# Two 32x32-block transposes moved past the inner product's additions, and three PSUM tiles at the end made smaller

## The chip, the cores and the metric

The kernel runs on one core of one Trainium2 chip, in one launch. The metric is the device time of one execution in microseconds. The kernel before took 2105.44 us, the median of three runs (2105.36 to 2105.63). Engines are named as the profile names them: PE is TensorE, DVE is VectorE, ACT is ScalarE, POOL is GpSimd and SP is SyncE, which issues the loads and stores here. PEld is PE's weight load.

## What is computed

Two layers on x (16 batches, 1024 nodes, 256 channels) in f32, with one adjacency matrix of 1024 by 1024 for all batches:

```python
# layer 0
c_adj = jnp.mean(fea, axis=1)                      # fea: x with channels first
diff = c_adj[:, None, :] - c_adj[:, :, None]
A = jnp.abs(jnp.abs(jax.nn.sigmoid(diff) - 0.5) - 0.5) * 2.0
A_s = (A + jnp.transpose(A, (0, 2, 1))) * 0.5
g = jax.nn.relu(jnp.einsum('bcn,bnm->bcm', fea, adj[None] * A_s) * para.reshape(1, C, N))
# q from g, k and v from x @ kv_w, 4 heads of 64
attn = jax.nn.softmax(jnp.einsum('bhnd,bhmd->bhnm', q, k) * scale, axis=-1)
x = _layernorm(x + jnp.einsum('bhnm,bhmd->bhnd', attn, v))
# layer 1, twice: loop + neighbours, 256 -> 128 -> 256
h = jax.nn.relu(x @ w1_loop + adj @ (x @ w1_neigh) + b1)
h = jax.nn.relu(h @ w2_loop + adj @ (h @ w2_neigh) + b2)
x = _layernorm(x + (x + h) * 0.5)
```

## The kernel before

One Python loop over the 16 batches lays out all instructions. The order on each engine is the order of the code, which is written by hand: there is no planner. What a tile waits for follows from its data and from its buffer: tiles of one tag take that tag's buffers in turn, and the next owner of a buffer waits until the last one has been read. PSUM has two tags: "big" (`big_psum`, L85, three buffers of two banks; `half_psum`, L88, takes one and uses half of it) and "bank" (`bank_psum`, L91, two buffers of one bank).

The batches are staggered. While batch b is in its attention, the first graph convolution runs for batch b - 1 (the object `c1`), the second for b - 2 (`c2`), and the last normalization for b - 3 (`c3`). Batches 2 to 14 share one branch (L1590 to L1649). Batches 3 to 14 have a `c3`; batch 2 has none. Batch 15 has its own branch (L1651 and L1731 on), as no batch follows it. After the loop, one more run and the ending serve what is left (from L1741).

In batches 2 to 14 the stage around the change goes like this:

- `att.both_units(0, ...)` (L828): scores of the first two of four units (PE, L769), exps (ACT, L776), their sums over the nodes (`collect`, DVE, L788 and L790), the products with v (PE, L815). The DVE part at its end, `settle`, is handed back and done later: a transpose of an av tile out of PSUM (L848) and a reduction (`part_sum`, L803). The function `summed` puts four sums (L1024 to L1027) and, where there is a `c3`, `deviation_aside` (DVE L1234, then POOL L1235, a power) ahead of that.
- `c1.fast_inner(...)` (L1032): x1 times the first layer's weights by Strassen's scheme with seven products of 128 by 512 on PE (L1037), in the order 1, 2, 7, 6, 3, 4, 5. They go to three half-used big PSUM tiles: `chain` takes 1, 6 and 5, `upper` takes 2 and 3, `lower` takes 7 and 4. ACT copies some of them out (L1043 to L1052), and DVE adds the others: L1045 reads `upper` after product 2, so product 3 waits for it; L1054 reads `lower` after product 4; L1056 and L1057 read `chain`; L1058 transposes the result, which SP then stores. Between L1045 and L1054 DVE does what `fast_inner` is handed as `aside`: `settle` and `turn_next`, the turn of next x from blocked to channel-major form, two transposes of 128x1024 (L253 in `channel_major`).
- `att.both_units(1, ...)`: the other two units in the same way. Its first score tiles take the big buffers that `upper`, `lower` and `chain` had, so the second of them waits for L1054. `third` of this call issues the ACT copy L880 behind its `settle`.
- `Joined.run` (L1385): both graph convolutions' products with the adjacency, also seven of them, in the order 1, 2, 6, 7, 5, 4, 3, with DVE work for other batches put between by `between`.

In batch 15 `fast_inner` has only `settle` as its `aside`. Its joined run ends with `c2.last_products` (L1181), seven products of which L1189 and L1196 add parts and `settle` (L1176, the line L1178) adds results to x. Its `between` puts `norm.scale` (L393, two DVE multiplications) behind product 4 and `norm.spread` (L395) behind product 3's relu: two transposes of x1 to channel-major form (L253) and eight stores of 128 KB each. L1449 is the addition that the relu (L1076) waits for. Then `c1.turn(0)` and `c1.turn(1)` turn h1 on PE (four transposes of 128x128 each, L1109) into a half-used big tile, and ACT copies it out (L1110). The last run begins with `c1.inner` for batch 15 (L1006), whose 32 products go to another big tile (L1011, `t_ps`) and are copied by ACT (L1014).

Of the kernel before, what the change touches and what calls it, by code (L numbers as in the profile page):

```python
# [10 lines left out]
F32 = mybir.dt.float32  # L11
# [7 lines left out]
def kernel(  # L19
# [31 lines left out]
    nc = tc.nc  # L51

    B, N, C = x.shape
    P = 128
    NT = N // P
    NC = C // P
# [22 lines left out]
    work = ctx.enter_context(tc.tile_pool(name="work", bufs=1))  # L79
# [169 lines left out]
    def channel_major(blocked, name):  # L249

        dst = work.tile([P, NC, N], F32, tag="xT", name=name, bufs=2)
        for cc in range(NC):
            nc.vector.transpose(dst[:, cc, :], blocked[cc])  # L253
        return dst
# [103 lines left out]
    class BlockedNorm:  # L358
# [31 lines left out]
        def scale(self):  # L390
            for cc in range(NC):
                x_cc = by_node(self.xB[cc])
                nc.vector.tensor_mul(x_cc, x_cc, self.rstd.unsqueeze(2).to_broadcast([P, NB, S]))  # L393

        def spread(self):  # L395
            self.x1T = channel_major(self.xB, f"x1T_{self.name}")
            self.nodes = nodes = dram.tile([N, C], F32, tag="x1d", name=f"x1d_{self.name}", bufs=3)
            for cc in range(NC):
                for a in range(Q):
                    c0 = cc * P + a * S  # L400
                    nc.sync.dma_start(out=nodes[:, c0:c0 + S].rearrange("(bn k) r -> k bn r", k=S),
                                      in_=by_node(self.xB[cc][a * S:(a + 1) * S, :]))
# [591 lines left out]
    class GraphConv:  # L994
# [34 lines left out]
            self.inner_factors = {1: (w1n_sb[:, 0, :], w11), 2: (w1n_sb[:, 1, :], w21), 3: (s4, w22),  # L1029
                                  4: (w1l_sb[:, 1, :], t4), 5: (s1, t1), 6: (s2, t2), 7: (s3, t3)}  # L1030

        def fast_inner(self, aside=lambda: None):  # L1032
            b = self.b

            def product(n, dst, again=False):
                w, xs = self.inner_factors[n]
                nc.tensor.matmul(dst, w, xs, start=not again, stop=True, skip_group_check=again)  # L1037

            upper, lower, chain = (half_psum(f"in_ps_{b}_{i}") for i in range(3))
            s12, s34, t1T, self.loops, t1B = (row_tile(f"in_{b}_{i}") for i in range(5))  # L1040
            p1, u2, p3, p7 = s12[:, 0:FB], s12[:, FB:N], s34[:, 0:FB], s34[:, FB:N]
            product(1, chain)
            nc.scalar.copy(p1, chain)  # L1043
            product(2, upper)
            nc.vector.tensor_add(t1T[:, 0:FB], p1, upper)  # L1045
            aside()
            product(7, lower)
            nc.scalar.copy(p7, lower)
            product(6, chain, again=True)
            nc.scalar.copy(u2, chain)  # L1050
            product(3, upper)
            nc.scalar.copy(p3, upper)  # L1052
            product(4, lower, again=True)
            nc.vector.tensor_add(self.loops[:, 0:FB], u2, lower)  # L1054
            product(5, chain, again=True)
            nc.vector.tensor_add(t1T[:, FB:N], p3, chain)  # L1056
            nc.vector.tensor_add(self.loops[:, FB:N], p7, chain)  # L1057
            nc.vector.transpose(t1B, t1T)  # L1058
            self.t1d = dram.tile([N, HID], F32, tag="t1d", name=f"t1d_{b}", bufs=2)
            for a in range(Q):  # L1060
                nc.sync.dma_start(out=self.t1d[:, a * S:(a + 1) * S].rearrange("(bn k) r -> k bn r", k=S),
                                  in_=by_node(t1B[a * S:(a + 1) * S, :]))
# [115 lines left out]
            nc.vector.scalar_tensor_tensor(rows, src.rearrange("p (t c) -> p t c", c=P), 0.0, rows,  # L1178
                                           op0=ALU.max, op1=ALU.add)

        def last_products(self, a, c):  # L1181
            name = f"h2_{self.b}"
            d = bank_psum(f"{name}_ps")
            snaps = [row_tile(f"{name}_{k}") for k in range(2)]
            p1, u2, u3 = snaps[0][:, 0:FB], snaps[0][:, FB:N], snaps[1][:, 0:FB]
            self.seventh_part(1, a)
            nc.scalar.copy(p1, a)
            self.seventh_part(2, d, start=True)
            nc.vector.tensor_add(p1, p1, d)  # L1189
            self.settle(0, 0, p1)  # L1190
            self.seventh_part(6, a)
            nc.scalar.copy(u2, a)
            self.seventh_part(5, c)
            self.seventh_part(7, a)
            nc.scalar.copy(u3, a)
            nc.vector.tensor_add(u3, u3, c)  # L1196

            def rest():
                self.settle(1, 1, u3)
                self.seventh_part(4, a)  # L1200
                self.settle(1, 0, a)
                self.seventh_part(3, c)
                nc.vector.tensor_add(u2, u2, c)
                self.settle(0, 1, u2)

            return rest
# [144 lines left out]
    class Joined:  # L1351
# [30 lines left out]
                nc.tensor.matmul(dst, self.x[n][:, k, :], of_rows(rows, k),  # L1382
                                 start=(start and k == 0), stop=(k == TJ - 1), skip_group_check=again)

        def run(self, between=None, last=None):  # L1385
            c1, c2, b = self.c1, self.c2, self.b
            between = between or {}

            def bias(bank, row):
                nc.scalar.copy(bank.rearrange("p (t c) -> p t c", c=P), row.unsqueeze(1).to_broadcast([P, TJ, P]))  # L1390

            def turn_to(n):
                for f in between.get(n, ()):
                    f()

            bigs = [big_psum(f"hu_ps_{b}_{i}") for i in range(3)]
            first, third, second = (big[:, 0:FB] for big in bigs)
            s12, s34 = (row_tile(f"snap_{b}_{k}") for k in range(2))
            p1, u1, u3, p7 = s12[:, 0:FB], s12[:, FB:N], s34[:, 0:FB], s34[:, FB:N]
            if c1.loops is None:  # L1400
                c1.loop(third, 0, start=True)
            else:
                nc.scalar.copy(third, c1.loops[:, 0:FB])
            self.product(1, first, start=True)
            nc.scalar.copy(p1, first)
            turn_to(1)
            self.product(2, third, again=c1.loops is not None)
            nc.vector.tensor_add(p1, p1, third)
            turn_to(2)
            if last and c2.w2 is None:  # L1410
                c2.load_sums()
            self.product(6, first, again=True)
            nc.scalar.copy(u1, first)
            c1.relu(0, p1)
            turn_to(6)
            self.product(7, second, start=True)
            nc.scalar.copy(p7, second)
            if last:
                bias(third, b2_sb[:, ts(0, P)])
            turn_to(7)  # L1420
            self.product(5, first, again=True)
            nc.scalar.copy(u3, first)
            turn_to(5)
            self.product(4, second, again=True)
            c2.uT = row_tile(f"uT_{c2.b}")
            add_upper = lambda: nc.vector.tensor_add(c2.uT[:, 0:FB], u1, second)
            add_lower = lambda: (last or nc.gpsimd).tensor_add(c2.uT[:, FB:N], u3, p7)
            if not last:
                add_upper()
                add_lower()  # L1430
                turn_to(4)
                c1.loop(first, 1, again=True)
                self.product(3, first, again=True)
                c1.relu(1, first)
                turn_to(3)
                return
            c2.block_sums(last, add_upper, add_lower)
            bias(second, c2.b2_step)
            turn_to(4)
            if c1.loops is None:  # L1440
                c1.loop(first, 1, again=True)
            self.product(3, first, again=True, steps=range(0, TJ // 2))
            rest = c2.last_products(third, second)
            self.product(3, first, again=True, steps=range(TJ // 2, TJ))
            if c1.loops is None:
                c1.relu(1, first)
            else:
                loop = c1.loops[:, FB:N]
                nc.vector.tensor_add(loop, loop, first)  # L1449
                c1.relu(1, loop)  # L1450
            turn_to(0)
            rest()
            turn_to(3)
            return third, second, bigs[1][:, FB:N], bigs[2][:, FB:N]

    def run():
# [59 lines left out]
        for b in range(B):  # L1516
# [73 lines left out]
            elif more:  # L1590
# [12 lines left out]
                    if c3:  # L1603
                        c3.deviation_aside()

                def turn_next():
                    nonlocal xT_next
                    xT_next = channel_major(blocked, f"xT_{b + 1}")

                xT_next = None  # L1610

# [8 lines left out]
                settle = att.both_units(0, sums, lambda: nodes.turn(), summed=summed)  # L1620
                nodes.line()
                nodes.row()
                c1.fast_inner(lambda: (settle(), turn_next()))
                att.both_units(1, before_convolution, third=lambda: (att.den_shift(), q.times_adj(0), q.times_adj(TJ), att.den_halves()))
                both.left(nc.gpsimd)
                q.left(nc.gpsimd, blocked)
# [103 lines left out]
            else:  # L1730
# [3 lines left out]
                both.left(nc.gpsimd)  # L1734
                both.fetch(1, 4, "11")
                both.run({1: (lambda: att.add_pairs(1), att.watch), 6: (norm.mean, norm.squares, norm.sum_squares),
                          5: (lambda: norm.variance(bank_psum),), 4: (norm.scale,), 0: (norm.spread,)}, last=nc.vector)
                c1.turn(0)
                c1.turn(1)
            convs[b] = GraphConv(b, norm.x1T, norm.nodes)  # L1740
        c1, c2, c3, c4 = (convs[B - k] for k in (1, 2, 3, 4))  # L1741
        both = Joined(c1, c2)
# [87 lines left out]
```

## Time and profile before

| | |
|---|---|
| median of three runs | 2105.44 us |
| the profiled execution: time, span | 2104.63 us, 2102.8 us |
| PE busy | 2090.7 us, 99% of the span |
| DVE busy | 1875.1 us, 89% |
| ACT busy | 1265.9 us, 60% |
| POOL busy | 425.5 us, 20% |
| mean granted PE clock | 0.999 |
| DMA | 364.99 MB, 174 GB/s |
| chain that ended last | PE 94%, DVE 4%, issue 1% |
| one 128x1024 transpose (L253) | 1.22 us, 62 of them |
| one batch of the steady part (b = 3 to 14) | 129.1 us |

The span reaches from the first to the last instruction that the profiler recorded; the execution's own time has 1.83 us around it. A row of the timeline gives start, length, engine, line, operation, the tile written and the tiles read with their shapes, how many instructions were put together in the row, and in brackets how long the engine was idle ahead of them and what ended the wait. Consecutive instructions overlap by some tenths of a microsecond, so that a row of two is shorter than twice one. A busy PE here means that a product is in its pipeline.

### The profile page before, as it was taken

The page shows a single profiled execution, that of the slowest core. Times are in us where ns is not written, and L with a number is a line of the kernel's source. Part 1 is how long each engine was busy: PE and PEld are TensorE (multiplying, and loading weights), DVE is VectorE, ACT ScalarE, POOL GpSimd, SP SyncE. Part 2 cuts the span into 40 slices and gives each one's busy share as a digit, 9 for nine tenths or more (in the row PEclk, how much of TensorE's full clock was granted, in tenths as well). Part 3 has the DMA queues.
Part 4 walks back from the last instruction along what each step waited for, and adds up shares of the span by engine and source line. Part 5 has one row for each costly group of instructions (what it writes and reads, how often), then busy time and mean ns, then how long its engine had stood idle before and what let it go on. Part 6 is the DMA issues. An engine that isn't in the chain of part 4 may idle for free.

```text
span 2102.8 us, 24938 instructions
## 1 busy us (share of the span) xinstructions
PE 2090.7 (99%) x8282; PEld 988.5 (47%) x8282; DVE 1875.1 (89%) x2238; ACT 1265.9 (60%) x2190; POOL 425.5 (20%) x444
## 2 busy tenths in 40 slices
PE   9999999999999999999999999999999999999998
PEld 5354434445354453544535444354443534445355
DVE  7899998989989899898998989899899998989875
ACT  5844575556756576565755757557575585655523
POOL 2011103122031221213122031220312203122022
PEclk9999999999999999999999999999999999999999
DMA  9495756766648776477864768656586674966455
GB/s 216 122 178 189 145 140 205 138 216 146 173 168 161 242 135 192 151 146 244 142 216 139 135 232 162 230 120 146 206 176 217 143 147 183 185 212 136 137 184 187
DMA packets 688695, 364.99 MB, mean 174 GB/s; under 512 B 550704, under 2 KB 629936, under 8 KB 688560
## 3 DMA queue, kind: packets, MB, share of 16 engines
q1 hardware_dynamic: 688288, 363.07, 66.8%
q8 instruction: 67, 1.10, 0.2%
q14 instruction: 68, 0.56, 0.1%
q10 hardware_dynamic: 272, 0.26, 0.0%
HBM read 305.46 MB, written 57.80 MB: 173 GB/s over the span
## 4 chain that ended last, share of the span: by engine, by line
PE 94%; DVE 4%; issue 1%; DMA 0%; ACT 0%; SPq 0%; DVEq 0%; POOLq 0%; POOL 0%
PE av L815 20%; PE s L769 20%; PE hu_ps L1382 17%; PE g_ps L714 16%; PE v_ps L475 5%; PE k_ps L471 5%; PE hu_ps L1174 4%; PE g_ps L633 3%; PE in_ps L1037 1%; DVE xT L253 1%; DVE den_part L803 1%; DVE acc L790 1%; PE h_ps L1085 1%; PE u_ps L1114 1%; PE h_ps L1174 1%
## 5 line engine op out<-in xcount | busy, mean ns | idle before, releaser
L790 DVE TENSOR_TENSOR acc<-acc,pr 128x1024 f32<-128x1024 f32 x384 | 481.3, 1253 | 34.0 <-ACT pr L776 0.5
L769 PE MATMUL s<-qT,kT 64*128 64x512 f32 x2048 | 452.2, 594 | 1.6 <-DVE in L1054 0.7
L815 PE MATMUL av<-pr,v 128*64 128x512 f32 x2048 | 447.0, 594 | 0.0
L776 ACT ACTIVATE pr<-s 128x1024 f32<-128x1024 f32 x392 | 392.7, 1119 | 60.0 <-PE s L769 60.0
L769 PEld LDWEIGHTS s<-qT,kT 64*128 64x128 f32 x2048 | 194.2, 187 | 247.1 <-issue 186.6
L815 PEld LDWEIGHTS av<-pr,v 128*64 128x64 f32 x2048 | 144.1, 137 | 297.3 <-issue 265.7
L1382 PE MATMUL hu_ps<-adj,R 128*128 128x512 f32 x480 | 213.6, 592 | 0.0
L625 DVE SCALAR_TENSOR_TENSOR wg<-wg,adj 128x1024 f32<-128x1024 f32 x128 | 167.9, 1350 | 3.6 <-ACT wg L620 3.6
L774 ACT ACTIVATE pr<-s 128x512 f32<-128x512 f32 x240 | 142.6, 705 | 0.0
L619 ACT ACTIVATE wg<-c_row,c_sums 128x1024 f32<-128x1024 f32 x120 | 139.4, 1162 | 3.0 <-DVE accB L797 1.0
L1382 PEld LDWEIGHTS hu_ps<-adj,R 128*128 128x128 f32 x480 | 90.0, 190 | 107.1 <-issue 105.7
L620 ACT ACTIVATE wg<-wg 128x1024 f32<-128x1024 f32 x128 | 135.4, 1057 | 4.1
L388 POOL TENSOR_TENSOR rstd<-rstd,neg_half 128x32 f32<-128x32 f32 x16 | 88.3, 5520 | 147.4 <-DVE rstd L385 146.3
L1235 POOL TENSOR_TENSOR rstd<-rstd,neg_half 128x8 f32<-128x8 f32 x12 | 19.7, 1640 | 440.4 <-DVE rstd L1234 440.4
L714 PE MATMUL g_ps<-wg,x 128*128 128x512 f32 x224 | 107.7, 593 | 0.0
L1373 POOL TENSOR_TENSOR R<-h 128x512 f32<-128x512 f32 x14 | 19.6, 1397 | 435.3 <-PE av L815 408.7
L1382 PE MATMUL hu_ps<-adj,t 128*128 128x512 f32 x240 | 107.1, 598 | 0.0
L714 PE MATMUL g_ps<-T,xB 128*128 128x512 f32 x208 | 106.2, 592 | 0.0
L714 PE MATMUL g_ps<-wg,xB 128*128 128x512 f32 x208 | 106.2, 592 | 0.0
L788 DVE TENSOR_TENSOR acc<-pr,pr 128x1024 f32<-128x1024 f32 x64 | 78.0, 1218 | 14.8 <-ACT pr L776 14.8
L797 DVE STREAM_TRANSPOSE accB<-acc 128x1024 f32<-128x1024 f32 x64 | 79.7, 1245 | 3.5 <-PE av L815 0.5
L880 ACT COPY den<-den_part 64x64 f32<-64x64 f32 x26 | 5.5, 210 | 122.7 <-DVE den_part L803 122.2
(316 smaller groups left out, 3339.3 us busy)
## 6 DMA issues: line engine op xcount, KB each, us to landing
adj<-adjT SPq DMA_DIRECT2D x210, 512.0 KB
adj<-in_adj_dram SPq DMA_DIRECT2D x128, 512.0 KB
para<-in_L_gnn_para_dram SPq DMA_DIRECT2D x32, 512.0 KB
xB_a<-in_x_dram SPq DMA_DIRECT2D x128, 128.0 KB
x1d<-xB_a SPq DMA_DIRECT2D x128, 128.0 KB
x<-x1d SPq DMA_DIRECT2D x16, 1024.0 KB
xB<-in_x_dram SPq DMA_DIRECT2D x120, 128.0 KB
x<-in_x_dram SPq DMA_DIRECT2D x15, 1024.0 KB
```

The source lines that it names most:

```text
L471: nc.tensor.matmul(dst, self.a[0][n], self.w[n], start=not again, stop=True, skip_group_check=again)
L475: nc.tensor.matmul(dst[:, ts(t, P)], self.w[n][:, ts(t, P)], self.a[1][n], start=not again and t == 0, stop=True, skip_group_check=again o ...
L619: nc.scalar.activation(wg, self.c_row, AF.Abs, bias=self.c_col[:, t:t + 1], scale=-1.0)
L620: nc.scalar.activation(wg, wg, AF.Tanh, scale=-0.5 / C)
L625: nc.vector.scalar_tensor_tensor(wg, wg, 1.0, self.adj.pop(t), op0=ALU.add, op1=ALU.mult)
L714: nc.tensor.matmul(self.p[n], x_n[:, k, :], w_n, start=(k == 0), stop=(k == TJ - 1))
L769: nc.tensor.matmul(halves[s], self.kT[rows, pair, ts(mt, P)], self.qT[rows, pair, ts(j, FB)], start=True, stop=True)
L774: nc.scalar.activation(pr[:, ts(s, FB)], halves[s], AF.Exp)
L776: nc.scalar.activation(pr, ps, AF.Exp)
L790: nc.vector.tensor_add(self.acc, self.acc, prs[mt])
L815: nc.tensor.matmul(pav[s * HD:(s + 1) * HD, :], self.v[:, mt, pair * P + s * HD:pair * P + (s + 1) * HD], prs[mt][:, ts(s, FB)], start=(mt ...
L1382: nc.tensor.matmul(dst, self.x[n][:, k, :], of_rows(rows, k), start=(start and k == 0), stop=(k == TJ - 1), skip_group_check=again)
```

## The change

In `fast_inner` a second hook, `early`, stands between product 2 and L1045. `turn_next` takes the halves that it is to turn.

- Batches 3 to 14: half 0 of next x is turned in `early`, ahead of L1045; half 1 is turned in `aside`, behind `settle`.
- Batch 2: both halves are turned behind `fast_inner`, that is behind L1058 and its stores.
- Batch 15: `last_products` is handed the turn of half 0 of x1 and puts it ahead of L1189; the settling of p1 that stood behind L1189 moves into `rest`, behind the turn of half 1. Half 1 and the eight stores stay where both halves were. The two PSUM tiles of h1's turn have the tag "bank" in place of "big".

```diff
+        def spread_half(self, cc):
+            if cc == 0:
+                self.x1T = work.tile([P, NC, N], F32, tag="xT", name=f"x1T_{self.name}", bufs=2)
+            nc.vector.transpose(self.x1T[:, cc, :], self.xB[cc])
+            if cc == NC - 1:
+                self.store_nodes()
+
         def spread(self):
             self.x1T = channel_major(self.xB, f"x1T_{self.name}")
+            self.store_nodes()
+
+        def store_nodes(self):
             self.nodes = nodes = dram.tile([N, C], F32, tag="x1d", name=f"x1d_{self.name}", bufs=3)
...
-        def fast_inner(self, aside=lambda: None):
+        def fast_inner(self, aside=lambda: None, early=lambda: None):
...
             product(2, upper)
+            early()
             nc.vector.tensor_add(t1T[:, 0:FB], p1, upper)
             aside()
...
-        def last_products(self, a, c):
+        def last_products(self, a, c, aside=None):
...
             self.seventh_part(2, d, start=True)
+            if aside:
+                aside()
             nc.vector.tensor_add(p1, p1, d)
-            self.settle(0, 0, p1)
+            if not aside:
+                self.settle(0, 0, p1)
...
             def rest():
+                if aside:
+                    self.settle(0, 0, p1)
                 self.settle(1, 1, u3)
...
-                def turn_next():
+                def turn_next(*ccs):
                     nonlocal xT_next
-                    xT_next = channel_major(blocked, f"xT_{b + 1}")
+                    if xT_next is None:
+                        xT_next = work.tile([P, NC, N], F32, tag="xT", name=f"xT_{b + 1}", bufs=2)
+                    for cc in ccs:
+                        nc.vector.transpose(xT_next[:, cc, :], blocked[cc])
...
-                c1.fast_inner(lambda: (settle(), turn_next()))
+                if c3:
+                    c1.fast_inner(lambda: (settle(), turn_next(1)), lambda: turn_next(0))
+                else:
+                    c1.fast_inner(settle)
+                    turn_next(0, 1)
...
-                          5: (lambda: norm.variance(bank_psum),), 4: (norm.scale,), 0: (norm.spread,)}, last=nc.vector)
-                c1.turn(0)
-                c1.turn(1)
+                          5: (lambda: norm.variance(bank_psum),), 4: (norm.scale,), 0: (lambda: norm.spread_half(1),)}, last=nc.vector,
+                         aside=lambda: norm.spread_half(0))
+                c1.turn(0, bank_psum)
+                c1.turn(1, bank_psum)
```

## The prediction

> **What bounds the kernel now.** I began with busy times: PE is busy 2090.7 of 2102.8 us, 99%, at full granted clock in every slice, and the chain that ended last is 94% PE and 4% DVE. So only two things can change the time: work taken off PE (the change takes none) or stretches in which PE waits. About 12 us of PE's span are not busy. Next I cut the chain to a batch in the middle (b = 5), which shows where DVE stands on it:
>
> ```profile
> 678.75 0.17 DVE in L1045
> ...
> 679.36 0.71 DVE o L848
> 680.07 1.10 DVE den_part L803
> 681.17 0.97 DVE xT L253
> ...
> 682.24 0.76 DVE xT L253
> ...
> 683.37 0.66 DVE in L1054
> ...
> 684.07 13.15 PE s L769 x60
> ```
>
> Start and length in us. From L1045 to L1054 DVE works without a gap, with the two turns of next x in it, and PE's scores wait for its end; after that the chain is PE to the end of the batch. The list of waits says how often:
>
> ```profile
> PEld s L769 <- DVE in L1054: 12.4, 13, 1.5
> ...
> DVE in L1045 <- PE in_ps L1037: 13.8, 13, 1.6
> ```
>
> Thirteen times (batches 2 to 14) a weight load of the scores waits, 12.4 us in all. And in the same batches DVE stands idle ahead of L1045. The timeline puts both on one clock, and the last batch, which has no next x to turn, shows the same stage without the two turns:
>
> ```profile
> 677.57 0.17 DVE L1234 TENSOR_SCALAR rstd<-mv 128x8 f32<-128x8 f32 x1
> 677.82 1.64 POOL L1235 TENSOR_TENSOR rstd<-rstd,neg_half 128x8 f32<-128x8 f32 x1 [36.69 <-DVE rstd L1234]
> 678.75 0.69 DVE L1045 TENSOR_TENSOR in<-in,in_ps 128x512 f32<-128x512 f32 x1 [1.02 <-PE in_ps L1037]
> 679.77 0.19 PEld L1037 LDWEIGHTS in_ps<-x1T,w_sums 128*128 128x128 f32 x1 [0.24 <-issue]
> 681.09 2.36 DVE L253 STREAM_TRANSPOSE xT<-xB 128x1024 f32<-128x1024 f32 x2
> 682.87 3.62 PE L769 MATMUL s<-qT,kT 64*128 64x512 f32 x14
> 684.07 0.30 PEld L769 LDWEIGHTS s<-qT,kT 64*128 64x128 f32 x4 [0.90 <-DVE in L1054]
> ```
> ```profile
> 1974.03 3.27 PE L769 MATMUL s<-qT,kT 64*128 64x512 f32 x14
> ```
>
> The same 14 score products take 3.62 us where the turns are in the way and 3.27 where they are not: 0.35 us is what the wait costs PE (most of the 0.90 us is cover, weights that would have been loaded ahead).
>
> **Batches 3 to 14: one turn goes ahead of L1045, one stays behind.** On DVE nothing is added; twelve times one 128x1024 transpose moves. I put PE's first inner product at 0 (676.66). Turn 0 can start when L1234 has issued, at 1.0. Its pitch is 1.15 (681.09 to 682.24 in the chain), so L1045 starts at about 2.15 in place of 2.09 and ends at 2.84. Behind L1045 on PE waits product 3, which overwrites what L1045 reads; its weight load is due at 3.11 (679.77), so 0.27 us are left and nothing is lost. Everything behind on DVE then comes one pitch less 0.06 earlier: L848, L803 and turn 1 start at 2.76, 3.39 and 4.49, and L1054 at 5.64 instead of 6.71, ending at 6.3. In the last batch L1054 starts at 5.52, as soon as its product is there, and the scores run at full pace; 0.12 us later still leaves 0.8 us before the second score tile is due at 7.17. So the wait of 0.90 goes and PE gains 0.35 us a batch. That it is kept behind the scores: in batch 15 the av products begin 20.14 us after the first inner product, in the others 20.49, so 0.35 passes through the exps; behind that PE's few waits (0.81 on its own av, 0.46 at L714, 0.76 at an av) hang on work that follows PE. DVE ends the pair with 1.36 us of idle time at L848, and its whole row of adds starts as much earlier as PE's. Turn 0 reads next x, whose loads have landed: the DMA engines move 0 GB/s from 677 to 684. The turns issue no DMA, and the order of SP, POOL, ACT and PE stays as it was; POOL's L1235 now has a transpose beside it instead of an idle DVE. SP's loads in the next stage change buffers with each other (one quarter of the adjacency no longer waits 5.5 us for DVE's L797 at 696.9, and a likeness tile waits there instead); the products that use them come at least 10 us after landing, so nothing. Sum: 12 x 0.35 = 4.2 us; from below 12 x 0.24 = 2.9, if only what the second score tile loses (7.41 against 7.17) comes back.
>
> **Batch 2: both turns behind the inner product.** DVE is late there (it has four sums ahead), L1045 ends at 3.80 and product 3 loses 0.3, which stays. With the turns gone from the middle, L1054 starts when its product is there, at 5.95 instead of 7.73, and the 1.5 us wait goes; the scores' first av, at 21.51, could come 0.93 earlier. But both turns, 2 x 1.15, now stand between L1058 and the first pair sum L788, which starts at 11.47 instead of 10.72. DVE's idle time ahead of L848 at the pair's end was 1.30; of this 0.75 and 0.93 go, leaving it 0.38 late, and L848 releases, by L803 and the ACT copies L880 and L1403, PE's second product of the joined run. So about 0.35 of the gain is lost there: 0.6 us, between 0 and 0.93.
>
> **The last batch's run.** One 128x1024 turn of x1 goes ahead of L1189, the settling of p1 goes behind, and h1's two turns on PE get one-bank tiles. The rows before:
>
> ```profile
> 2032.73 2.37 DVE L253 STREAM_TRANSPOSE x1T<-xB_a 128x1024 f32<-128x1024 f32 x2
> ...
> 2033.71 0.60 PE L1109 MATMUL h1n_ps<-ident,h1T 128*128 128x128 f32 x4
> 2034.99 0.66 PE L1109 MATMUL h1n_ps<-ident,h1T 128*128 128x128 f32 x4 [0.68 <-ACT h L1110]
> 2036.32 3.84 PE L1011 MATMUL t_ps<-w1n_sb,x1T 128*128 128x128 f32 x32 [0.68 <-ACT h L1110]
> ```
>
> All three groups use one PSUM buffer in turn, so PE waits twice for ACT's copy L1110 (0.58 us). With two banks, h1n_1 follows h1n_0 after four products at 0.11, at 2034.15, and t_ps at 2034.6 if x1's second turn is done: alone it runs from 2032.73 to 2033.93. So t_ps starts 1.7 us earlier (the two idle stretches alone are 1.36; with the weight loads behind them 1.8). Turn 0 takes 2029.02 to 2030.2; L1189 then ends at 2030.86 instead of 2029.70, ahead of L1196 at 2031.03, which waits for ACT as before; settling p1, 0.6 more on DVE behind 2035, is less than the 1.15 that turn 0 took away. The stores of x1, eight of 128 KB on SP, come 1.2 us earlier in an unchanged order. PE's next need is the copy of t (ACT, 1.01, beside four L1070 products of 1.88, as now), and then the adjacency: its least slack, from landing to use, is 2.7 us in the rows, so 1.0 remains. Gain 1.7 us, from below 0.7 if a store or a later load takes that slack and 1.0 more, from above 1.8.
>
> **Sum.** 4.2 + 0.6 + 1.7 = 6.5 us off the profiled execution, 2104.63 us (span 2102.8 and 1.83 around it): 2098.1. The median of the three runs is 0.81 above the profiled one, so 2098.9 us, 0.31% faster. The bounds give 2.9 + 0 + 0.7 = 3.6 to 4.2 + 0.93 + 1.8 = 6.9: 2101.8 to 2098.5.
>
> **Rivals.** *The early turn makes product 3 wait (slower).* DVE's idle gap is 1.02 and the turn needs 1.15, and POOL's L1235 runs from 677.82 to 679.46 beside it. Elsewhere a DVE add beside POOL stretches, and a transpose beside POOL does not:
>
> ```profile
> 705.04 3.40 DVE L790 TENSOR_TENSOR acc<-acc,pr 128x1024 f32<-128x1024 f32 x2
> 706.04 1.31 POOL L1373 TENSOR_TENSOR R<-h 128x512 f32<-128x512 f32 x1 [26.59 <-PE av L815]
> 707.43 2.14 POOL L1374 TENSOR_TENSOR R<-R,t 128x512 f32<-128x512 f32 x1
> 708.54 1.25 DVE L797 STREAM_TRANSPOSE accB<-acc 128x1024 f32<-128x1024 f32 x1
> ```
>
> The pair of adds takes 3.40, in batch 15 without POOL 2.55. Were the turn stretched by the same 0.85, L1045 would be 0.91 late and product 3 0.64 late, a net loss of 0.29 a batch: 12 x 0.29 - 2.3 = +1.2, 2106.6. Were it held until POOL is done, it would end at 680.66, product 3 would wait some 1.55, and the net would be +1.2 a batch: 12 x 1.2 - 2.3 = +12.1, 2117.5. It costs from 0.27 us of delay on, and is slower by more than 0.2% from 1.16 on. Against it stands the last row: 1.25, with L1374 running beside it to 709.57, against a mean of 1.245 for L797. The Trainium skill, "SBUF — State Buffer", section "Who interferes with whom", has GpSimd share one pair of ports with VectorE under an exclusive lock, but says that a VectorE instruction with one SBUF input (outside the two-port modes) doesn't take it; both rows here agree. By its lock alone, taken for a transpose too, the sum would be the +12.1 above, by its exception -6.5.
>
> *The scores' wait goes, and another takes its place (within 0.2%).* If PE's 0.35 a batch is given back, to the exps or at the pair's end, only batch 2 and the end are left: -2.3, 2103.1; with half of it kept 2101.0. The exps do hold PE at other places, 25.7 us in 98 waits, but batch 15 keeps its 0.35 through them.
>
> *The end is bound by loads.* The DMA engines are full there, at 408 GB/s from 2040 to 2050. Then 1.7 shrinks to 0.7 or nothing: 2099.9 to 2100.6, still faster.
>
> That the moved turns stay where they were is excluded: DVE's instruction order in the changed kernel has turn 0 right behind L1234.
>
> **How the numbers follow.** 0.2% of 2105.44 is 4.2 us, about what measuring tells from no change. The forecast, with the end bound by loads as part of it, 0.78, 2098 to 2101; the wait replaced 0.11; the turn stretched 0.03; the turn held, or a delay that nothing here shows, 0.08. Faster needs less than 2101.2: the 0.78 and a little of the second, 0.79. Within 0.2%: 0.13, slower: 0.08. The range goes from 2097.6 (the upper bounds and 0.9 for what they miss) to 2103.2, the replaced wait's value, and leaves out about 0.15.
>
> **What would show it.** In the changed profile: turn 0 directly behind L1234 at 1.20; the idle time ahead of L1045 gone; no wait of the scores for L1054; 14 score products in 3.27; av at 20.14 after the first inner product. In batch 2, L788 at 11.5 and DVE without idle time ahead of L848. At the end, no L1109 row with a wait, and t_ps 1.7 us sooner after the last L1174 group. Wrong would be: a new wait of in_ps's product 3 on L1045, a transpose of 2 us, an adjacency load that ends a PE wait in the last run.

## The result, and the profile after

The changed kernel takes 2099.34 us, the median of eight runs (2098.87 to 2099.61), against 2105.59 (2105.06 to 2106.34): 6.25 us less, a ratio of 0.9971 with a 95% interval of 0.9961 to 0.9981. The forecast was 2098.9. The profiled execution has a span of 2097.7 us and a time of 2099.46; PE is busy 2087.8 us of it.

The stage of batch 5 again, from the timeline of the changed kernel, DVE, POOL, one weight load and the scores (start, length, engine, line, operation; in brackets the idle time ahead and what ended it). L1250, L1056, L1065, L1627 and L779 are here what L1234, L1045, L1054, L253 and L769 were; PE's first inner product starts at 675.54:

```profile
676.45 0.16 DVE L1250 TENSOR_SCALAR rstd<-mv 128x8 f32<-128x8 f32 x1
676.52 1.24 DVE L1627 STREAM_TRANSPOSE xT<-xB 128x1024 f32<-128x1024 f32 x1
676.69 1.64 POOL L1251 TENSOR_TENSOR rstd<-rstd,neg_half 128x8 f32<-128x8 f32 x1 [36.70 <-DVE rstd L1250]
677.68 0.65 DVE L1056 TENSOR_TENSOR in<-in,in_ps 128x512 f32<-128x512 f32 x1
...
678.65 0.19 PEld L1047 LDWEIGHTS in_ps<-x1T,w_sums 128*128 128x128 f32 x1 [0.24 <-issue]
...
679.98 1.23 DVE L1627 STREAM_TRANSPOSE xT<-xB 128x1024 f32<-128x1024 f32 x1
681.13 0.65 DVE L1065 TENSOR_TENSOR in<-in,in_ps 128x512 f32<-128x512 f32 x1
...
681.74 5.84 PE L779 MATMUL s<-qT,kT 64*128 64x512 f32 x25
```

The first turn fills the gap behind L1250, and L1056 has no idle time left ahead of it; it starts 2.14 us after the first inner product, where it was 2.09. Product 3's weight load comes at 3.11, as before. L1065 starts at 5.59 instead of 6.71, and the scores run without a break, 25 products in one row. The av products begin 20.14 us after the first inner product instead of 20.49, in each of the twelve batches, and from one batch to the next it is 128.77 us instead of 129.11.

The end, from the timeline of PE: first the products of the adjacency with t in the kernel before, then the changed kernel:

```profile
2041.71 7.03 PE L1382 MATMUL hu_ps<-adj,t 128*128 128x512 f32 x16
```
```profile
2029.10 1.04 PE L1120 MATMUL h1n_ps<-ident,h1T 128*128 128x128 f32 x8
2029.97 3.74 PE L1021 MATMUL t_ps<-w1n_sb,x1T 128*128 128x128 f32 x32
2033.55 1.88 PE L1081 MATMUL hu_ps<-x1T,w1l_sb 128*128 128x512 f32 x4
2035.27 7.61 PE L1398 MATMUL hu_ps<-adj,t 128*128 128x512 f32 x16
```

h1's eight transposes are one group now, and the products of t follow them at once. But the sixteen products of the adjacency with t take 7.61 us where they took 7.03. The list of waits, PE's weight loads, names a cause that was smaller before (1.4 us in 6 waits, none over 0.2); 0.91 and 0.75 of the 4.1 us are in the last run:

```profile
PEld hu_ps L1398 <- DMA adj<-adjT: 4.1, 12, 0.9
```

From batch 2's first inner product to batch 15's it is 1674.75 us instead of 1679.52 (4.77 less), from there to the last product of PE 126.45 instead of 127.70 (1.25 less). Ahead of batch 2 0.16 were lost. From the last product's start the final stores and the end of the program take 8.0 us instead of 7.3. SP's last two stores account for it:

```profile
2098.38 1.06 SPq L1349 DMA_DIRECT2D out_dram<-x  x2
```
```profile
2092.52 1.77 SPq L1365 DMA_DIRECT2D out_dram<-x  x2
```

So the profiled span falls by 5.2 us (2102.8 to 2097.7). The median falls by 6.25 because the profiled execution of the kernel before was 0.96 faster than the median of its eight runs, and that of the changed kernel 0.12 slower. Which part of the program differs so from one execution to the next is not shown.

### The profile page after: what moved, and what is told of

It is laid out like the page before. It is cut to its first block, busy times and chain, and to the rows that moved or that the text cites. A ratio compares the mean times of both kernels' runs of the same rounds, so it can differ in the third digit from the quotient of the medians.

```text
span 2097.7 us, 24950 instructions
## 1 busy us (share of the span) xinstructions
PE 2087.8 (100%) x8282; PEld 992.8 (47%) x8282; DVE 1877.3 (89%) x2238; ACT 1264.6 (60%) x2190; POOL 427.0 (20%) x444
## 5 line engine op out<-in xcount | busy, mean ns | idle before, releaser
L779 PE MATMUL s<-qT,kT 64*128 64x512 f32 x2048 | 448.8, 593 | 0.0
L779 PEld LDWEIGHTS s<-qT,kT 64*128 64x128 f32 x2048 | 198.4, 187 | 238.0 <-issue 188.4
L1398 PE MATMUL hu_ps<-adj,R 128*128 128x512 f32 x480 | 213.6, 592 | 0.0
L635 DVE SCALAR_TENSOR_TENSOR wg<-wg,adj 128x1024 f32<-128x1024 f32 x128 | 168.7, 1356 | 3.6 <-ACT wg L630 3.6
L1398 PEld LDWEIGHTS hu_ps<-adj,R 128*128 128x128 f32 x480 | 89.9, 190 | 107.2 <-issue 104.7
L1251 POOL TENSOR_TENSOR rstd<-rstd,neg_half 128x8 f32<-128x8 f32 x12 | 19.7, 1640 | 440.4 <-DVE rstd L1250 440.4
L1398 PE MATMUL hu_ps<-adj,t 128*128 128x512 f32 x240 | 107.8, 600 | 0.2
```

Source lines behind the costliest of these rows:

```text
L635: nc.vector.scalar_tensor_tensor(wg, wg, 1.0, self.adj.pop(t), op0=ALU.add, op1=ALU.mult)
L779: nc.tensor.matmul(halves[s], self.kT[rows, pair, ts(mt, P)], self.qT[rows, pair, ts(j, FB)], start=True, stop=True)
```

## The experiments

"The changed kernel" stands for the kernel with the whole change. All intervals are 95%, against the kernel before, run beside it.

### Batches 3 to 14 alone

```diff
                 if c3:
                     c1.fast_inner(lambda: (settle(), turn_next(1)), lambda: turn_next(0))
                 else:
-                    c1.fast_inner(settle)
-                    turn_next(0, 1)
+                    c1.fast_inner(lambda: (settle(), turn_next(0, 1)))
```
with the last batch as in the kernel before.

> Batches 3 to 14 alone are changed: turn 0 ahead of L1045, turn 1 behind settle; batch 2 and the end are as before. My theory (PE loses 0.35 us a batch to the wait for L1054, and keeps it when the wait goes): 12 x 0.35 = 4.2 us less than before, 2101.4, period of the steady batches 128.77 in place of 129.11. Rival (what the scores gain is given back at the pair's end, so that the end and batch 2 carry the change): within 1 us of before, period 129.11.

2101.28 us against 2105.46, 4.18 less, ratio 0.9979 (0.9970 to 0.9988). The period (from one batch's first inner product to the next one's) is 128.77, av begins at 20.14, and the rest of the program has its old times. The rival falls: nothing is given back at the pair's end. Two thirds of the whole gain come from here.

### Batch 2 alone

```diff
                 if c3:
-                    c1.fast_inner(lambda: (settle(), turn_next(1)), lambda: turn_next(0))
+                    c1.fast_inner(lambda: (settle(), turn_next(0, 1)))
                 else:
                     c1.fast_inner(settle)
                     turn_next(0, 1)
```

> Batch 2 alone is changed: both turns behind the inner product. My theory: the scores' av 0.93 us earlier, 0.35 of it lost again because L848 comes late; 0.6 us less than before, 2105.0, and the first inner product of batch 3 130.13 - 0.6 = 129.5 us behind that of batch 2. Rival (the late turns cost nothing): 0.93 less, 129.2. Rival (they cost all): 130.1.

2105.15 against 2105.46, ratio 0.9999 (0.9990 to 1.0008): the time can't tell it from nothing. The trace can: batch 3 begins 129.54 us behind batch 2 in place of 130.13 to 130.15, 0.6 less. The first av comes 0.94 earlier (20.57 for 21.51), and 0.35 of it is lost, as expected. In the changed kernel's timeline of that batch DVE's L858 has no idle time ahead of it any more, and a weight load of the joined run waits for ACT's copy behind it. The last two adds ahead of L858, first in the kernel before, then in the changed kernel:

```profile
317.76 3.40 DVE L790 TENSOR_TENSOR acc<-acc,pr 128x1024 f32<-128x1024 f32 x2
```
```profile
318.58 3.91 DVE L800 TENSOR_TENSOR acc<-acc,pr 128x1024 f32<-128x1024 f32 x2
...
323.77 0.68 DVE L858 STREAM_TRANSPOSE o<-av 128x512 f32<-128x512 f32 x1
...
326.69 0.30 PEld L1398 LDWEIGHTS hu_ps<-adj,t 128*128 128x128 f32 x2 [0.91 <-ACT hu_ps L1419]
```

The amount agrees with the forecast, the way to it does not quite. L858 comes 0.73 later than its av tile allows (35.31 us after the first inner product; with idle time ahead of it, in the last experiment but one, 34.58), and not 0.38: the first of the two adds now runs beside POOL's L1390 and takes 1.70 us instead of 1.18. The weight load shown comes 0.67 behind the 0.43 us pitch of the loads ahead of it, but the products behind it only 0.35, as the load otherwise runs 0.43 ahead of its product.

### The last batch: all of it, the PSUM tiles alone, the turns alone

The PSUM tiles that change are the two of h1's turn (two, where the title says three). The whole of the end, with batches 2 to 14 as before:

```diff
-                if c3:
-                    c1.fast_inner(lambda: (settle(), turn_next(1)), lambda: turn_next(0))
-                else:
-                    c1.fast_inner(settle)
-                    turn_next(0, 1)
+                c1.fast_inner(lambda: (settle(), turn_next(0, 1)))
```

> The last batch alone is changed: x1's turns apart and h1 in one-bank tiles. From the changed kernel's trace: the products of t start 1.74 us earlier, L1070 and the first adjacency product 1.83, and then an adjacency load comes late, 0.58 us, so that 1.25 us stay: 2104.3. If the late load was chance in that one profile: 1.8 us, 2103.8. If the loads are the limit in each execution, the wait of the first adjacency products for DMA is there again with 0.5 to 0.7 us.

2103.83 against 2105.46, 1.63 less, ratio 0.9991 (0.9982 to 1.0000).

Of it the one-bank tiles alone (the edits of this and the next against the kernel above):

```diff
-                          5: (lambda: norm.variance(bank_psum),), 4: (norm.scale,), 0: (lambda: norm.spread_half(1),)}, last=nc.vector,
-                         aside=lambda: norm.spread_half(0))
+                          5: (lambda: norm.variance(bank_psum),), 4: (norm.scale,), 0: (norm.spread,)}, last=nc.vector)
                 c1.turn(0, bank_psum)
                 c1.turn(1, bank_psum)
```

> Only h1's two PSUM tiles of the last batch change, from the big buffers to the one-bank ones; x1's turns stay together. The second turn of x1 ends at 2035.10 in the trace of before, so the products of t can start 1.2 us earlier instead of 1.74. With my theory of a load with 1.45 us to spare at its last of 16 parts, no load is late at 1.2, so this alone gains 1.2 us, as much as with the turns apart: 2104.2. Rival (the turns have to be apart for a gain): 0 to 0.5 us.

2104.23, 1.23 less, ratio 0.9994 (0.9985 to 1.0003).

And the turns apart alone:

```diff
-                c1.turn(0, bank_psum)
-                c1.turn(1, bank_psum)
+                c1.turn(0)
+                c1.turn(1)
```

> Only x1's turns of the last batch stand apart; h1's PSUM tiles stay in the big buffers. My theory (the end's gain comes from the tiles): the products of t start 68.5 us after the last batch's first inner product as in the kernel before; no change, 2105.5. Rival (the turns hold them): 1.2 to 1.7 us less.

2104.68 against 2105.51, 0.8 less, ratio 0.9996 (0.9987 to 1.0005); I had expected nothing. By these intervals neither half alone can be told from nothing. Times in the last batch, counted in each trace from its first inner product, tell the steps apart better than the medians (R is a sum of h and t that DVE makes for the joined run):

| | products of t begin | first adjacency product | first product with R |
|---|---|---|---|
| before | 68.49 | 73.89 | 80.75 |
| turns apart alone | 67.98 | 73.38 | 80.24 |
| tiles alone | 66.76 | 72.50 | 79.37 |
| both (end alone) | 66.77 | 72.06 | 79.27 |
| the changed kernel | 66.76 | 72.05 | 79.50 |
| the changed kernel, second profile | 66.77 | 72.06 | 79.66 |

The tiles take away both waits for ACT. With them, the products of t begin even with the second turn unfinished, as only the second half of each sum reads it: PE's row of the tiles-alone kernel shows a wait of 0.18 us after two products.

```profile
2034.63 0.39 PE L1021 MATMUL t_ps<-w1n_sb,x1T 128*128 128x128 f32 x2
2035.20 3.62 PE L1021 MATMUL t_ps<-w1n_sb,x1T 128*128 128x128 f32 x30 [0.18 <-DVE x1T L253]
```

Having the turns apart is worth 0.44 on top (72.50 to 72.06), of which 0.1 is left at the first product with R, as a load is now late. Alone it is worth 0.51, by another way than its name says: in that kernel the products of t wait for DVE's settling (L1189) and not for the second copy of h1. I read from this that their tile moved to the big buffer that the settlings read.

```profile
2036.03 3.17 PE L1021 MATMUL t_ps<-w1n_sb,x1T 128*128 128x128 f32 x26 [0.15 <-DVE x L1189]
```

### How late may L1056 come? One and a half turns, and two, ahead of it

```diff
-                    c1.fast_inner(lambda: (settle(), turn_next(1)), lambda: turn_next(0))
+                    c1.fast_inner(lambda: (settle(), nc.vector.transpose(xT_next[:, 1, FB:N], blocked[1][:, FB:N])),
+                                  lambda: (turn_next(0), nc.vector.transpose(xT_next[:, 1, 0:FB], blocked[1][:, 0:FB])))
```

> As the changed kernel, but in batches 3 to 14 one and a half turns stand ahead of L1045 and the last half (128x512) behind settle. By the same 0.28 us to spare: L1045 0.6 later, product 3 waits 0.32, 12 x 0.32 = 3.9 us more than the changed kernel, 2103.2: nearly all that the early turn brought is gone. If there is more to spare than 0.6: 2099.3.

```diff
-                    c1.fast_inner(lambda: (settle(), turn_next(1)), lambda: turn_next(0))
+                    c1.fast_inner(settle, lambda: turn_next(0, 1))
```

> As the changed kernel, but in batches 3 to 14 both turns stand ahead of L1045. My theory (L1045 has some 0.28 us to spare before product 3 waits): L1045 starts 1.15 later, at 3.30 after the first product, product 3 waits 0.87, and PE is later by as much in each batch: 12 x 0.87 = 10.4 us more than the changed kernel, 2109.8, slower than before. Rival (product 3 has other cover, or the time comes back later in the batch): within 2 us of the changed kernel.

One and a half: 2101.28 us (2100.47 to 2103.68), ratio to before 0.9980 (0.9971 to 0.9989). Two: 2107.52, ratio 1.0007 (0.9998 to 1.0016). But the periods are 128.79 and 129.33, so that the turns cost 0.02 and 0.56 us a batch, not 0.32 and 0.87. Both timelines of batch 5, first with one and a half turns (first inner product at 676.35), then with two (676.86):

```profile
679.12 0.65 DVE L1056 TENSOR_TENSOR in<-in,in_ps 128x512 f32<-128x512 f32 x1
...
679.82 0.30 PEld L1047 LDWEIGHTS in_ps<-x1T,w_sums 128*128 128x128 f32 x2 [0.59 <-DVE in L1056]
679.89 1.06 PE L1047 MATMUL in_ps<-x1T,w_sums 128*128 128x512 f32 x2
```
```profile
680.16 0.65 DVE L1056 TENSOR_TENSOR in<-in,in_ps 128x512 f32<-128x512 f32 x1
...
680.86 0.30 PEld L1047 LDWEIGHTS in_ps<-x1T,w_sums 128*128 128x128 f32 x2 [1.13 <-DVE in L1056]
680.86 1.12 PE L1047 MATMUL in_ps<-x1T,w_sums 128*128 128x512 f32 x2 [0.30 <-DVE in L1056]
```

The weight load of product 3 normally runs 0.43 us ahead of its product (3.11 and 3.54). With one and a half turns it comes at 3.47, still ahead of 3.54, and the product starts on time. With two turns it comes at 4.00 and the product with it. So L1056 has 0.6 us to spare and not 0.28: the load's cover belongs to it. Between the two kernels L1056 comes 0.53 us later (2.77 and 3.30), and the period is 0.54 longer: from there on its delay is paid in full. The medians are larger than the periods say, by 1.6 and 1.4 us; that is a cost of another kind (below, SP's last branch).

### Both turns behind the inner product in all batches

```diff
-                    c1.fast_inner(lambda: (settle(), turn_next(1)), lambda: turn_next(0))
+                    c1.fast_inner(settle)
+                    turn_next(0, 1)
```

> As the changed kernel, but batches 3 to 14 turn both halves behind the inner product as batch 2 does. The scores' wait is gone here too (the second score tile at 7.17). My theory: the first pair sum L798 starts 1.65 later, at 11.0; DVE has 1.30 of idle time ahead of L858, so it comes 0.35 late and PE's second product of the joined run waits as in batch 2: 12 x 0.35 = 4.2 us more than the changed kernel, 2103.5. Rival (only the wait of the scores counts, the place behind is free): 2099.3.

2105.42 against 2105.60: as slow as before, ratio 1.0000 (0.9991 to 1.0009). av begins at 20.14, the scores keep their 0.35, and the first pair sum starts at 11.00; but the period is 129.11 to 129.12, again what it was before, with one batch of 129.43. The 0.35 a batch is lost at the pair's end. From the timeline of batch 5:

```profile
711.26 0.67 DVE L858 STREAM_TRANSPOSE o<-av 128x512 f32<-128x512 f32 x1
...
713.54 0.59 ACT L1419 COPY hu_ps<-in 128x512 f32<-128x512 f32 x1
714.18 0.30 PEld L1398 LDWEIGHTS hu_ps<-adj,t 128*128 128x128 f32 x2 [0.91 <-ACT hu_ps L1419]
```

L858 comes 34.88 us after the first inner product, where the changed kernel has it at 34.14 with 1.30 us of idle time ahead: 0.74 late and not 0.35, again because an add runs beside POOL (1.70 instead of 1.18 us), and again PE loses less than that, 0.34. So the place counts, not that the turns are out of the way: behind the inner product DVE's row has no room for 1.65 us. In batches 3 to 14 this rival of the change is worth nothing, for the reason by which batch 2's gain was cut. Its median holds a further cost, which hides what batch 2 and the end bring (below, SP's last branch).

### The stores of x1 behind the adjacency loads

```diff
         def spread_half(self, cc):
...
-            if cc == NC - 1:
-                self.store_nodes()
+            self.nodes = None
...
         both.fetch("00", "10", 2, 3)
+        norm.store_nodes()
+        c1.nodes = norm.nodes
```

> As the changed kernel, but the eight stores of the last batch's x1 stand on SP behind the first eight adjacency loads of the last run instead of ahead of them. My theory (these loads land at a set time behind the stores, and the end's gain is cut to 1.25 by them): the wait of the first adjacency products for DMA goes, 0.6 us less than the changed kernel, 2098.7, and the products of t to the first product with R take 12.7 us as in the kernel before instead of 13.2. Rival (the loads wait for their buffers, not for the stores): no change, 2099.3, the waits stay.

2099.04 us in six runs, ratio to before 0.9970 (0.9957 to 0.9982), 0.3 to 0.4 below the changed kernel's 2099.34 and 2099.47, which the runs can't tell from none. In the trace the wait is gone. PE's rows of this kernel, and of the changed kernel in its second profile:

```profile
2035.16 7.03 PE L1397 MATMUL hu_ps<-adj,t 128*128 128x512 f32 x16
```
```profile
2035.88 1.88 PE L1398 MATMUL hu_ps<-adj,t 128*128 128x512 f32 x4
2038.23 5.42 PE L1398 MATMUL hu_ps<-adj,t 128*128 128x512 f32 x12 [0.47 <-DMA adj<-adjT]
```

The first product with R comes 78.92 us after the batch's first inner product, the full 1.83 earlier than before; the other kernel with the stores there (next but one) has 78.92 too. With the stores ahead it was 78.92 once (both turns late), and 79.27 to 80.32 in the six other profiles with both turns apart and one-bank tiles. So with the stores ahead the loads hold PE up by varying amounts, 0 to 1.4 us; they stand behind stores that keep the DMA engines busy at 0.97 while they move 141 GB/s.

### The changed kernel again

> The changed kernel once more, to be compared with the others of this call: 2099.3 us.

2099.47 us against 2105.51, 6.04 less, ratio 0.9972 (0.9962 to 0.9983).

### Batch 2's turns behind the second pair

With the stores placed as in the experiment above:

```diff
                     c1.fast_inner(settle)
-                    turn_next(0, 1)
-                att.both_units(1, before_convolution, third=lambda: (att.den_shift(), q.times_adj(0), q.times_adj(TJ), att.den_halves()))
+                att.both_units(1, before_convolution, third=lambda: (att.den_shift(), None if c3 else turn_next(0, 1), q.times_adj(0), q.times_adj(TJ), att.den_halves()))
```

> As the changed kernel with x1's stores of the last batch behind the first adjacency loads, and batch 2's two turns behind the settling of its second pair (ahead of the products with the adjacency's quarters) in place of behind the inner product. My theory: batch 2 keeps all of its 0.93 (batch 3's first product 129.2 behind batch 2's), no load is waited for at the end: some 0.8 us less than the changed kernel, 2098.5. Rival (the turns are as dear there, since DVE then comes late to the joined run's first addition): 129.5, 2098.9.

2100.55, ratio to before 0.9978 (0.9969 to 0.9987): 1.1 slower than the changed kernel, and neither theory gave that. L858 has its idle time back (1.24), but batch 3 begins 130.80 us behind batch 2, 1.26 later than in the changed kernel. From the timeline, DVE, ACT and PE (L634, L1420 and L1397 are L635, L1421 and L1398 of the changed kernel):

```profile
327.50 3.59 DVE L634 SCALAR_TENSOR_TENSOR wg<-wg,adj 128x1024 f32<-128x1024 f32 x2
331.16 0.58 ACT L1420 COPY snap<-hu_ps 128x512 f32<-128x512 f32 x1 [4.77 <-PE hu_ps L1397]
331.85 2.38 PE L1397 MATMUL hu_ps<-adj,R 128*128 128x512 f32 x5 [1.35 <-issue]
```

ACT's copy starts 0.07 us behind the end of DVE's two products with the adjacency (331.09); in the changed kernel it is 0.08, at 329.44. The next group on PE writes into the tile that ACT copies, and starts 0.1 behind it. So DVE's two products were the next work with a date, and the turns pushed them past it. That ACT waits for them is read from these ends, in four places; which buffer makes it wait I did not settle.

### The place of SP's last branch

At the program's end all engines take a branch over a fallback part. The groups of the branch's line on SP, first the eight waits behind the branch and then the branch, with their times, in the kernel with both turns late:

```profile
L1800 SPq EVENT_SEMAPHORE  x8: 17/17/17, 2100.7 to 2101.3; - x8
...
L1800 SPq COMPARE_BRANCH  x1: 50/50/50, 2098.2 to 2098.2; - x1
```

From the branch's end to the next instruction SP takes 2.48 us there. In all traces it goes by the number of SP's instructions that the trace has ahead of the branch: 1747 (before, batches 3 to 14 alone, the end alone and its two halves) 0.44; 1746 (the changed kernel, batch 2 alone, and the two with the stores moved) 0.78 to 1.06; 1734 (one and a half turns, two turns, both late) 2.48 to 2.70. In the last three a dozen waits stand on ACT's queue instead of SP's. To test it I added 13 instructions to the late one, by cutting two loads:

```diff
+        if name in ("9", "10"):
+            for t in range(NT if name == "9" else NT - 2):
+                nc.sync.dma_start(out=xb[:, t, :], in_=x[b, t * P:(t + 1) * P, :])
+            if name == "10":
+                nc.sync.dma_start(out=xb[:, NT - 2:NT, :], in_=x[b, (NT - 2) * P:N, :].rearrange("(t p) c -> p t c", p=P))
+            return xb
         nc.sync.dma_start(out=xb, in_=x[b].rearrange("(t p) c -> p t c", p=P))
```

> The kernel with both turns behind the inner product in batches 3 to 14, with two loads of x (1 MB each, long before use) cut into 8 and 7 parts, so that SP has 13 instructions more and its last branch stands where it stands in the kernel before. There SP goes on 0.44 us behind that branch, without the 13 instructions 2.5 us. If the place of the branch in SP's code decides: 0.44 again, and 2 us less than without, 2103.4. If the place of the turns or chance does: 2.5, and 2105.4.

2103.84, ratio to before 0.9992 (0.9983 to 1.0001), 1.6 us less than without the 13 instructions. SP goes on 0.44 us behind the branch:

```profile
L1806 SPq EVENT_SEMAPHORE  x8: 17/17/17, 2101.2 to 2101.7; - x8
...
L1806 SPq COMPARE_BRANCH  x1: 50/50/50, 2100.7 to 2100.7; - x1
```

The place of the branch in SP's code decides how long SP stands. What the program pays is less: the last store lands 0.7 to 1.0 us behind the branch, and in five of the six profiles with 0.44 the third of the eight waits ends only with that landing. From the branch's end to the end of the span it is 2.74 us in the kernel before (0.44) and 2.72 in the changed kernel's first profile (0.78), 2.97 in its second (1.06), and 4.39 to 4.61 in the three with 2.48 to 2.70. So the branch costs these three 1.4 to 1.9 us more than the changed kernel, and that agrees with what their medians have above their periods: one and a half turns 2101.28 = 2099.4 + 12 x 0.02 + 1.6, two turns 2107.52 = 2099.4 + 12 x 0.56 + 1.4, both late 2105.42 = 2099.4 + 12 x 0.34 + 1.9.

## Why the prediction was right, and where it wasn't

| step | predicted | trace of the changed kernel | alone, medians |
|---|---|---|---|
| batches 3 to 14 | 4.2 | 4.18 | 4.18 |
| batch 2 | 0.6 | 0.59 | 0.3 |
| the end | 1.7 | 1.25 | 1.63 |
| the program's end | 0 | -0.7 | |
| ahead of batch 2 | 0 | -0.16 | |
| sum | 6.5 | 5.16 | 6.1; whole change 6.25 |

The median came out at 2099.34 where 2098.9 was forecast, and that closeness is in part luck. The forecast of the profiled execution, 2098.1, was 1.4 us too low (2099.46), because the end gave 0.45 less than its term, the program's end took 0.7 and the stretch ahead of batch 2 0.16 that were put at nothing. The forecast then carried over that the median lies 0.81 above the profiled execution, as in the kernel before; in the changed kernel it lies 0.12 below.

- *Batches 3 to 14.* Right in size and in mechanism. The turn takes 1.24, L1056 is 0.05 late, L1065 comes at 5.59 (forecast 5.64), av at 20.14. What made the figure sure was that the last batch already ran the stage without the turns: its 0.35 was a measurement and no estimate. One sentence is too wide: not everything behind L1045 comes earlier. L848 and L803 stay where they were (2.72 and 3.34 for 2.70 and 3.33); L1054 and what follows come earlier.
- *The margin of product 3.* Too small in the prediction: "0.27 us are left". I took the start of the weight load for the date, but a load ahead of time is cover. Measured, 0.6 are left. The forecast didn't hang on it, the price of the slower rivals did: the stretched turn would have cost some 0.3 a batch, not 0.64, and would have left the kernel faster than before.
- *POOL beside the turn.* The rivals with POOL fall: the turn takes 1.24 us beside POOL's L1251, as much as the other at 1.23, and L1251 takes 1.64 in all twelve batches before and after. The Trainium skill's exception for an instruction with one SBUF input ("SBUF — State Buffer", section "Who interferes with whom") holds here. The test is a mild one, as L1251 works on 128x8 elements.
- *Batch 2.* Right in size: 0.94 from the scores, 0.35 lost because DVE comes late to the pair's end. The second figure is right by luck: two things were left out that nearly cancel, the add that POOL stretches (L858 is 0.73 late where 0.38 was forecast) and the weight load that runs ahead of its product. The experiment with all batches showed that the loss is not particular to batch 2. The median alone shows only 0.3, but this kernel also ends later: from the end of the last product on it takes 7.80 us in its profile, the kernel before 7.15.
- *The end.* The waits for ACT's copies go as forecast (1.74 earlier at t, 1.83 at the first adjacency product). The term that was mis-sized is the loads' slack: "its least slack, from landing to use, is 2.7 us in the rows, so 1.0 remains". I had taken earlier parts of a load for its end, and the product for its use. The last part of the tightest load lands 1.45 us ahead of the weight load that needs it (2043.27 and 2044.72 in the trace of before), so 1.83 was too much for it. The rival "the end is bound by loads" thus came true for 0.58 us of the 1.83, and with it one of the prediction's own signs of being wrong, an adjacency load that ends a PE wait in the last run; with the stores behind the loads, neither shows.
- *The program's end.* Not in the prediction. Two parts make the 0.7. Ahead of the last store SP stands idle for 0.34 us instead of 0.06; it does so in all five profiles with 1746 instructions ahead of the branch and in none of the nine others (0.05 to 0.06), so that this too seems to go by the place in SP's code, which no run tested apart. And SP takes 1.02 us to issue the last store instead of 0.62, which differs from profile to profile (0.62 to 1.38). The branch itself adds nothing there: 2.72 us from it to the end, and 2.74 before.

The medians of the three parts sum to 6.1 us, the whole change to 6.0 and 6.25: as far as medians with intervals of 2 us to each side can tell, the parts don't help or hinder each other. No version ran that is clearly better than the changed kernel; the one with the stores behind the loads is as fast or 0.4 us faster.

## What to carry to other kernels

Before moving an instruction into an engine's idle gap, look for a batch or an iteration that lacks it: its rows give the gain without an estimate. Then check the next date on that engine in both directions, and whether what moves later there comes to run beside another engine that stretches it; here one turn ahead fits, one and a half just fit, two don't, and two behind give everything back some 25 us later. For a transfer's slack take the last part to land and the weight load, not the product, and for a product's slack add the time that its weight load runs ahead.

## What the runs showed of the hardware that I had not expected

- SP's last branch takes 0.44, 0.78 to 1.06 or 2.5 to 2.7 us until SP goes on, by its place in the code: 13 instructions more made 2.48 into 0.44. Two otherwise equal kernels so differ by 1.6 us in the median, 0.1% here and as much as the whole change of the last batch brought. Below 1 us it is covered by the last store's landing: with 0.44 and with 0.78 the program ends alike (2.74 and 2.72 us behind the branch). The Trainium skill, "Runtime: NRT & Kernel Launch", section "Instruction fetch mechanics", says that a taken branch whose target lies outside the pages held at that moment has to wait for their fetch. The three groups of times agree with that; where the pages end is shown by no run.
- A weight load of f32 (128 by 128, 0.19 us) runs 0.43 us ahead of its product, beside the product before it, and may come 0.36 late at no cost (one and a half turns ahead of L1056: 0.02 us a batch).
- Stores that move 141 GB/s keep the DMA engines as busy (0.97) as loads at 396 to 411 GB/s (1.00 to 1.03), and the first product that needs R comes 0 to 1.4 us late behind such loads, by the profile.
